# Moving loads of S, own rows and the diagonal to GpSimd's queue, two writes to ScalarE's, and dealing the first layer out sooner

## The chip, the cores and the metric

The kernel runs on one core of a Trainium2 chip. The metric is the device time of one execution in microseconds, given as the median of several runs. The core has five engines that each run their own instruction list in order: TensorE (PE in the profile; its weight loads are PEld), VectorE (DVE), ScalarE (ACT), GpSimd (POOL) and SyncE (SP). Transfers are issued by an engine's list and are carried out by 16 DMA engines that all lists share. In the profile the list of SP is SPq.

## The reference, cut to what matters

The input x has 32 batches of 512 nodes with 256 features; adj is one sparse 512 x 512 matrix whose pattern is symmetric. Four layers follow one another. The first and the last have this form:

```python
pre_u = einsum('bud,dk->buk', h_t, W1[:d])
pre_v = einsum('bvd,dk->bvk', h_t, W1[d:])
hidden = relu(pre_u[:, :, None, :] + pre_v[:, None, :, :] + b1)
S = sigmoid(einsum('buvk,ko->buvo', hidden, W2)[..., 0] + b2[0])
a_t = einsum('buv,bud->bvd', S * A_a, h_t)
m_t = einsum('uv,bud->bvd', A_m, h_t) * h_t
z_t = beta1*h_t + beta2*(a_t @ Wa + ba) + beta3*(m_t @ Wm + bm)
```

Both matrices A_a and A_m are adj, so S is needed only where adj is not zero. The second layer is z + relu(adj z W + b); the third is an attention layer over all 512 x 512 pairs, with adj added to its logits.

## The kernel before

The 32 batches are worked in 8 groups of 4 (t = 0 to 7). For each group, and for the first layer ("0") and the last ("3") apart, there is a table in device memory with the rows pre_u and pre_v of every node for the 4 batches (2 MB), and a grid "cells" of 512 x 512 x 4 values of S * adj, in two halves.

**The streams.** `sparse_path` gives each group five streams of pieces, each a Python generator:

- `first` (21 pieces): loads h, transposes it into hT (`turned`, L537), writes hT to xT in device memory (L730), and in `pre` makes the table rows (L549 on DVE, L550 on ACT) and writes them (table<-puv, L557).
- `edges` of layer 0: works through ITEMS = 36 lists of 128 adjacency entries. Each item fetches 128 rows of the table by an indirect DMA on GpSimd (rows<-table, L582), adds the node's own rows (`mine`, a plain load of 512 KB, L622, four per run, in DVE L654), forms relu times W2 and sums it (DVE L667), takes the sigmoid and puts 128 x 4 values into cells by an indirect DMA on GpSimd (cells<-s, L576). Each put waits until the put before it to the same half has landed. The diagonal of cells is written apart (`own_1`, L606).
- `middle`: loads S * adj from cells (SA, four loads of 1 MB, `load`, L689), then goes through the 4 batches: rest of layer 0, layers 1 and 2, the table of layer 3. It writes x2T (L876) and x2 (L888). The attention's output is yT, in two halves (DVE L874), and `pre` of layer 3 needs both of them.
- `edges` of layer 3, and `last`: the rest of layer 3, which loads SA again, and x2 and x2T, and writes the output.

**Their order.** `weave` sorts all pieces by a due time in units of one group and emits them in that order. Pieces of kind "fill" (`first`, `last`) are held back, up to HELD = 8 of them while a `middle` runs, and are let out at places that `middle` marks. The order on each engine is then set by the framework's scheduler, which goes by its own estimates of time. An instruction that waits holds up everything behind it on its engine, and the same holds for the DMA issues in an engine's list.

**Who issues what.** In the kernel before, SP issues every plain transfer. GpSimd issues only the indirect ones. Buffers that matter here: hT has one buffer, which `first` and `last` share; puv has three, `mine` three, rows five, SA four for each layer.

For t from 2 on, `first` and then `edges` of layer 0 of group t come before its `start`, while `middle` of group t-1 runs; `edges` of layer 3 and `last` of a group come behind its `end`, as the numbers `early` and `behind` tell. So during `middle` of group t-1 the run of `edges` of layer 3 of group t-2 comes first, and that of layer 0 of group t follows it.

There is also a dense path for matrices with too many entries; it is not taken here.

Of the kernel before, what the change touches and what calls it, by code (L numbers as in the profile page):

```python
# [16 lines left out]
P = 128  # L17
# [28 lines left out]
class Model:  # L46
# [37 lines left out]
    def load(self, name, shape, view, pool=None):  # L84
        t = (pool or self.const).tile(shape, F32, name=f"w_{name}")
        self.nc.scalar.dma_start(t, view)
        return t
# [327 lines left out]
class Sparse:  # L415
# [24 lines left out]
    def psum(self):  # L440
        return self.ps.tile([P, N], F32, name="pst", tag="pst")
# [144 lines left out]
    def edges(self, g, spare=()):  # L586

        nc, e, w = self.nc, self.e, g.w  # L590
        flat = "p c b -> p (c b)"
        own = g.self_s.rearrange(flat)
        ready, fetched = [], {}
        lead = LEAD + len(spare) - 1 if spare else LEAD
        tags = [None] * 5 + list(spare)
        mine = {}
        places = g.table.rearrange("(c p k) n -> c k p n", p=P, k=2)

        def own_1():
            self.sigmoid_of(own)  # L600
            diag = self.counts.diag.unsqueeze(2).to_broadcast([P, NC, NB])
            nc.vector.tensor_tensor(g.self_s, g.self_s, diag, ALU.mult)
            for q in range(2):
                diagonal = g.cells[q][q * HALF : q * HALF + HALF * (N + 1), :]
                diagonal = diagonal.rearrange("(c p a) b -> p c a b", p=P, a=N + 1)[:, :, 0, :]
                nc.sync.dma_start(diagonal, g.self_s[:, 2 * q : 2 * q + 2, :])  # L606

        def run_1(ks):
            self.sigmoid_of(g.s[:, ks, :].rearrange(flat))
            value = e.value[:, ks].unsqueeze(2).to_broadcast([P, ks.stop - ks.start, NB])  # L610
            nc.vector.tensor_tensor(g.s[:, ks, :], g.s[:, ks, :], value, ALU.mult)
            for k in range(ks.start, ks.stop):
                j = e.order[k]
                ready.append((e.half_of(j), e.cell[:, j : j + 1], g.s[:, k, :]))

        def fetch(n):
            j = e.order[n]
            c = j // OWN
            if c >= NC or c not in mine:
                t = self.gath.tile([P, GROUP], F32, name="mine", bufs=3)  # L620
                if c < NC:
                    nc.sync.dma_start(t, places[c, 0])  # L622
                    mine[c] = t
                else:
                    self.fetch(t, g, e.iu[:, j - NC * OWN : j - NC * OWN + 1])
            else:
                t = mine[c]
            if tag := tags[n % len(tags)]:
                rows = self.act.tile([P, GROUP], F32, name="rows_more", tag=tag)
            else:  # L630
                rows = self.gath.tile([P, GROUP], F32, name="rows")
            self.fetch(rows, g, e.iv[:, j : j + 1])
            fetched[n] = rows, t

        def put():

            at = next((n for n, r in enumerate(ready) if r[0] != self.half), 0)
            if ready:
                r = ready.pop(at)
                self.half = r[0]  # L640
                self.put(g, *r)

        self.half = 1
        for n in range(lead):
            fetch(n)
        yield

        todo = [(2, lambda: self.exp_of(w, own)), (4, own_1)]
        done = 0
        for k in range(ITEMS):  # L650
            for _ in range(2 if spare and len(ready) > 2 else 1):
                put()
            rows, other = fetched.pop(k)
            nc.vector.tensor_tensor(rows, rows, other, ALU.add)  # L654
            if k + lead < ITEMS:
                fetch(k + lead)
            if spare:
                by_entry = rows.rearrange("p (b d) -> p b d", b=NB)
                w2 = w["W2bc"].unsqueeze(1).to_broadcast([P, NB, D])
                nc.vector.scalar_tensor_tensor(by_entry, by_entry, 0.0, w2, ALU.max, ALU.mult)  # L660
            for b in range(NB):
                part = rows[:, b * D : (b + 1) * D]
                at = g.s[:, k, b : b + 1]
                if spare:
                    nc.scalar.activation(part, part, AF.Identity, accum_out=at)
                else:
                    nc.vector.scalar_tensor_tensor(part, part, 0.0, w["W2bc"], ALU.max, ALU.mult, accum_out=at)  # L667
            if k % 4 == 3 or k >= ITEMS - 3:
                ks = slice(done, k + 1)
                near = spare or k >= ITEMS - 5  # L670
                todo.append((k + (1 if near else 3), lambda ks=ks: self.exp_of(w, g.s[:, ks, :].rearrange(flat))))
                todo.append((k + (1 if near else 4), lambda ks=ks: run_1(ks)))
                done = k + 1
            while todo and todo[0][0] <= k:
                todo.pop(0)[1]()
            yield
        for _, f in todo:
            f()
        while ready:
            put()  # L680
        yield

    def load(self, g, layer):

        tiles = []
        for c in range(NC):
            t = self.act.tile([P, N, NB], F32, name=f"SA{layer}", bufs=NC)
            cells = g.cells[c // 2][c % 2 * P * N : (c % 2 + 1) * P * N, :]
            self.nc.sync.dma_start(t.rearrange("p v b -> p (v b)"), cells.rearrange("(p v) b -> p (v b)", p=P))  # L689
            tiles.append(t)  # L690
        return tiles

# [24 lines left out]
    def first(self, g, i):  # L717


        def load(b):  # L720
            h = self.act.tile([P, NC, D], F32, name="h0", tag="h", bufs=2)
            self.nc.sync.dma_start(h, self.xr[i + b])
            return h

        h = load(0)
        for b in range(NB):
            ahead = load(b + 1) if b < NB - 1 else None
            hT = self.turned(h, "hT0", "hT")
            yield
            self.nc.sync.dma_start(self.xT[i + b], hT)  # L730
            yield from self.pre(g, b, hT)
            h = ahead
        self.settle()
# [53 lines left out]
    def middle_one(self, g0, g3, b, i, SA, keep, given):  # L787
        nc, m, w = self.nc, self.m, g0.w
        act, small, psum = self.act, self.small, self.psum
        h, hT, hWa, flat = keep  # L790
# [89 lines left out]
        for c in range(0, NC, 2):  # L880
            pt = psum()
            for k in range(2):
                for d in range(DC):
                    at = k * D + d * P
                    nc.tensor.transpose(pt[:, at : at + P], xT[:, d, (c + k) * P : (c + k + 1) * P], m.ident)
            x2 = small.tile([P, 2, D], F32, name="x2", tag="ex", bufs=4)
            nc.scalar.copy(x2, by_two(pt))
            nc.sync.dma_start(self.x2s[i][:, c : c + 2, :], x2)  # L888
            yield

    def put_back(self, eT, ic, ex):
# [116 lines left out]
def sparse_path(ctx, m, counts, xr, outr, B):  # L1008
# [10 lines left out]
    for t in range(last + 1):  # L1019
        g0, g3 = Group(sp, m.g0, f"0_{t}"), Group(sp, m.g3, f"3_{t}")  # L1020
        start, end = (max(0.0, k - 0.47) for k in (t, t + 1))
        behind = (end, end + 0.48), (end + 0.52, end + 1.2)
        if t == 0:
            early = (-0.385, -0.30), (-0.292, -0.02)
        elif t == 1:
            early = (-0.28, -0.06), (0.02, start - 0.04)
        else:
            early = (start - 0.8, start - 0.54), (start - 0.53, start - 0.05)
        if t == last - 1:
            behind = (end, end + 0.46), (end + 0.6, end + 1.08)  # L1030
        if t == last:
            end -= 0.2
            behind = (end, end + 0.46), (end + 0.29, end + 0.45)
        streams += [
            (sp.first(g0, t * NB), FIRST, *early[0], "fill"),
            (sp.edges(g0, ("yT", "mhT3") if t == 0 else ()), EDGES, *early[1], ""),
            (sp.middle(g0, g3, t * NB), middle_shares(t == 0), start, end, "main"),
            (sp.edges(g3, ("yT", "h1", "hT1") if t == last else ()), EDGES, *behind[0], "free"),
        ]
        if t == 0:  # L1040
            streams.append((sp.middle_before(g0, 0), AHEAD, -0.15, -0.03, ""))
        if t < last:
            streams.append((sp.last(g3, t * NB), LAST, *behind[1], "fill"))
        else:
            streams.append((sp.last_before(g3, t * NB), AHEAD, *behind[1], ""))
            streams.append((sp.last_behind(g3, t * NB), BEHIND, end + 0.5, end + 0.6, ""))
# [235 lines left out]
```

## Time and profile before

| | |
|---|---|
| median of 3 runs | 3247.94 us (3246.24 to 3251.05) |
| profiled execution | 3230.9 us, span from first to last instruction 3229.2 us |
| PE / DVE / POOL / ACT busy | 2773.2 / 2371.6 / 1488.3 / 1007.0 us |
| mean granted TensorE clock | 0.928 |
| DMA by GpSimd's queue / SP's queue | 338.90 MB / 334.68 MB |
| busy share of the 16 DMA engines, same queues | 32.8% / 31.0% |

One period of the steady state is about 371 us. In it PE is busy for nine tenths of the time, and DVE is full while an `edges` run is on. Lines such as L557 are lines of the kernel before; the change keeps the line numbers. In a list of waits, "A <- B: x, n, y" says that A waited for B for x us in all, n times, at most y us. In the chain of waits each row has its start, its length and what ran or was waited for.

### The profile page before, as it was taken

The numbers are of one execution on the slowest core, as the hardware profiler recorded it, in microseconds if no ns is written. First come the engines' busy times: TensorE is split into PE (matmuls) and PEld (weight loads), VectorE is DVE, ScalarE is ACT, GpSimd is POOL, SyncE is SP. The second block draws the span as 40 slices with busy tenths as digits, with TensorE's granted clock in tenths as the row PEclk, the third lists the DMA queues.
The fourth block names the chain that finished last, engine by engine and source line by source line (L and its number), as shares of the span: only waits on it lengthen the run. The fifth ranks groups of instructions, "written<-read, shape, count | busy, mean of one in ns | idle before, by whom it ended". The sixth has DMA issues, their size and how long they took to land.

```text
span 3229.2 us, 32451 instructions
## 1 busy us (share of the span) xinstructions
PE 2773.2 (86%) x8646; PEld 1656.2 (51%) x8646; DVE 2371.6 (73%) x7692; ACT 1007.0 (31%) x2341; POOL 1488.3 (46%) x1248
## 2 busy tenths in 40 slices
PE   6346887989997999979999899979998899999947
PEld 3223444546554566435654565536654465545626
DVE  7777736989596976969598786969688695953662
ACT  4452333322233222333223232333223222232441
POOL 1565402747264543636354462636355362630371
PEclk9677898999999999989999999989999999999969
DMA  8876425777567766776577766776577765640663
GB/s 273 295 246 229 152 91 166 261 262 224 188 226 240 234 196 202 249 241 220 173 230 235 245 203 211 237 250 207 178 219 246 242 221 190 219 159 33 209 201 112
DMA packets 302718, 679.40 MB, mean 210 GB/s; under 512 B 52672, under 2 KB 170944, under 8 KB 294336
## 3 DMA queue, kind: packets, MB, share of 16 engines
q0 software_dynamic: 111168, 338.90, 32.8%
q1 hardware_dynamic: 186224, 334.68, 31.0%
q10 hardware_dynamic: 5136, 3.68, 0.4%
q8 instruction: 71, 1.16, 0.1%
q14 instruction: 119, 0.97, 0.1%
HBM read 531.12 MB, written 146.01 MB: 210 GB/s over the span
## 4 chain that ended last, share of the span: by engine, by line
PE 38%; DVE 34%; DMA 17%; issue 6%; ACT 3%; POOL 1%; SPq 0%; ACTq 0%; POOLq 0%; DVEq 0%
PE pst L43 28%; DVE rows L667 11%; DVE rows L654 10%; DMA rows<-table,iv 6%; DMA table<-puv 4%; PE pst L945 4%; PE pst L802 2%; DMA cells<-s,cell 2%; PE pst L954 1%; DVE ex L852 1%; PE pst L896 1%; DMA cells<-self_s 1%; PE pst L809 1%; DVE ex L854 1%; DMA mine<-table,iu 1%
## 5 line engine op out<-in xcount | busy, mean ns | idle before, releaser
L582 POOL DMA_INDIRECT rows<-table,iv x554 | 680.1, 1228 | 1047.4 <-DMA table<-puv 383.1
L576 POOL DMA_INDIRECT cells<-s,cell x576 | 684.3, 1188 | 592.7 <-DMA cells<-s,cell 357.0
L654 DVE TENSOR_TENSOR rows<-rows,mine 128x1024 f32<-128x1024 f32 x554 | 667.3, 1215 | 195.0 <-DMA rows<-table,iv 178.9
L667 DVE SCALAR_TENSOR_TENSOR rows<-rows,L_gnn_W2bc 128x256 f32<-128x256 f32 x2016 | 750.9, 413 | 0.4
L43 PE MATMUL pst<-adj,h 128*128 128x512 f32 x1024 | 453.5, 592 | 0.0
L43 PE MATMUL pst<-L_gnn_Wa,hT 128*128 128x256 f32 x1024 | 260.6, 408 | 142.4 <-DMA hT<-xT 69.4
L43 PE MATMUL pst<-w_L_gnn_W,hT 128*128 128x512 f32 x512 | 261.2, 646 | 57.4 <-ACT hT L537 46.3
L43 PEld LDWEIGHTS pst<-adj,h 128*128 128x128 f32 x1024 | 192.8, 190 | 219.5 <-issue 214.1
L43 PEld LDWEIGHTS pst<-L_gnn_Wa,hT 128*128 128x128 f32 x1024 | 207.8, 208 | 187.8 <-issue 103.2
L43 PE MATMUL pst<-w_L_gnn_W,yT 128*128 128x512 f32 x512 | 239.9, 622 | 66.0 <-DVE yT L874 66.0
L43 PE MATMUL pst<-eT,feats 128*128 128x512 f32 x512 | 240.0, 624 | 9.1 <-ACT eT L897 9.1
L43 PE MATMUL pst<-adjT,zW 128*128 128x512 f32 x512 | 225.9, 592 | 0.0
L550 ACT COPY puv<-pst 128x256 f32<-128x256 f32 x256 | 94.7, 372 | 412.5 <-DVE puv L549 376.2
L945 PEld LDWEIGHTS pst<-hWa,SA 128*128 128x128 f32 x896 | 213.4, 328 | 5.9 <-issue 3.3
L945 PE MATMUL pst<-hWa,SA 128*128 128x256 f32 x896 | 216.2, 397 | 0.0
L43 PEld LDWEIGHTS pst<-w_L_gnn_W,yT 128*128 128x128 f32 x512 | 101.8, 200 | 196.3 <-issue 111.0
L549 DVE TENSOR_TENSOR puv<-pst,bc_L_gnn_b 128x256 f32<-128x256 f32 x256 | 106.6, 417 | 127.4 <-PE pst L43 64.4
L771 ACT COPY flat<-SA 128x512 f32<-128x512 f32 x128 | 134.5, 1122 | 203.3 <-PE pst L43 178.8
L802 PE MATMUL pst<-flat,hWa 128*128 128x512 f32 x448 | 196.8, 592 | 0.0
L43 PEld LDWEIGHTS pst<-w_L_gnn_W,hT 128*128 128x128 f32 x512 | 102.0, 206 | 168.0 <-issue 90.5
L43 PE MATMUL pst<-WT,hT 128*128 128x256 f32 x512 | 141.8, 434 | 38.8 <-DVE hT L810 38.8
L896 PE MATMUL pst<-ident,ex 128*128 128x128 f32 x512 | 88.5, 302 | 99.2 <-DVE ex L857 62.6
(167 smaller groups left out, 3728.0 us busy)
## 6 DMA issues: line engine op xcount, KB each, us to landing
table<-puv SPq DMA_DIRECT2D x256, 256.0 KB, 4.9
SA<-cells SPq DMA_DIRECT2D x64, 1024.0 KB, 7.0
h<-in_x_dram SPq DMA_DIRECT2D x64, 512.0 KB, 6.6
mine<-table SPq DMA_DIRECT2D x64, 512.0 KB, 6.2
hT<-xT SPq DMA_DIRECT2D x36, 512.0 KB, 5.0
h<-x2s SPq DMA_DIRECT2D x36, 512.0 KB, 6.1
xT<-hT SPq DMA_DIRECT2D x32, 512.0 KB, 7.5
x2T<-yT SPq DMA_DIRECT2D x32, 512.0 KB, 5.0
```

The source lines that it names most:

```text
L43: nc.tensor.matmul(out, lhsT, rhs, start=(n == 0), stop=(n == len(pairs) - 1))
L549: nc.vector.tensor_tensor(puv[:, 0, :], pp[:, 0:D], w["b1bc"], ALU.add)
L550: nc.scalar.copy(puv[:, 1, :], pp[:, D:])
L576: self.nc.gpsimd.indirect_dma_start(out=g.cells[half], out_offset=bass.IndirectOffsetOnAxis(ap=at, axis=0), in_=s, in_offset=None)
L582: self.nc.gpsimd.indirect_dma_start(out=rows, out_offset=None, in_=g.table, in_offset=bass.IndirectOffsetOnAxis(ap=at, axis=0))
L654: nc.vector.tensor_tensor(rows, rows, other, ALU.add)
L667: nc.vector.scalar_tensor_tensor(part, part, 0.0, w["W2bc"], ALU.max, ALU.mult, accum_out=at)
L771: self.nc.scalar.copy(flat[:, r, :], SA[r][:, :, b])
L802: nc.tensor.matmul(pz, hWa[:, r, cs], flat[:, r, :], start=(r == 0), stop=False)
L809: nc.tensor.matmul(pz, w["Wm"][:, d, cs], mhT[:, d, :], start=False, stop=(d == DC - 1))
L896: nc.tensor.transpose(pt[:, js], ex[:, js], self.m.ident)
L945: nc.tensor.matmul(pz[:, k * D : (k + 1) * D], SA[r][:, cs, b], hWa[:, r, :], start=(r + k == 0), stop=False)
```

## The change

Five issues change their engine, and two numbers of the order change. 160 transfers go from SP to GpSimd (64 loads of SA, 64 of `mine`, 32 of the diagonal) and 96 from SP to ScalarE (32 writes of xT, 64 of x2). `first` of group t >= 2 gets due times 0.06 of a group sooner, and `last` has to be through 0.07 of a group sooner.

```diff
-                nc.sync.dma_start(diagonal, g.self_s[:, 2 * q : 2 * q + 2, :])
+                nc.gpsimd.dma_start(diagonal, g.self_s[:, 2 * q : 2 * q + 2, :])
...
-                    nc.sync.dma_start(t, places[c, 0])
+                    nc.gpsimd.dma_start(t, places[c, 0])
...
-            self.nc.sync.dma_start(t.rearrange("p v b -> p (v b)"), cells.rearrange("(p v) b -> p (v b)", p=P))
+            self.nc.gpsimd.dma_start(t.rearrange("p v b -> p (v b)"), cells.rearrange("(p v) b -> p (v b)", p=P))
...
-            self.nc.sync.dma_start(self.xT[i + b], hT)
+            self.nc.scalar.dma_start(self.xT[i + b], hT)
...
-            nc.sync.dma_start(self.x2s[i][:, c : c + 2, :], x2)
+            nc.scalar.dma_start(self.x2s[i][:, c : c + 2, :], x2)
...
-        behind = (end, end + 0.48), (end + 0.52, end + 1.2)
+        behind = (end, end + 0.48), (end + 0.52, end + 1.13)
...
-            early = (start - 0.8, start - 0.54), (start - 0.53, start - 0.05)
+            early = (start - 0.86, start - 0.6), (start - 0.53, start - 0.05)
```

## The prediction

> **What bounds the kernel now.** I read the page first: busy times, then the chain that ended last.
>
> ```profile
> PE 2773.2 (86%) x8646; PEld 1656.2 (51%) x8646; DVE 2371.6 (73%) x7692; ACT 1007.0 (31%) x2341; POOL 1488.3 (46%) x1248
> ...
> PE 38%; DVE 34%; DMA 17%; issue 6%; ACT 3%; POOL 1%; SPq 0%; ACTq 0%; POOLq 0%; DVEq 0%
> ```
>
> PE is nearest to a bound, with 456 us idle in 3229.2 us. No queue move makes PE's work smaller, so a gain can only come out of that idle time. Busy time by stretches puts 146 us of it into the first 320 us (set-up) and 63 us into the last 209 us. In the steady state it sits in one place per group: where `edges` of layer 3 ends and `edges` of layer 0 of the next group but one begins. Six such stretches of 56 us:
>
> ```profile
> 1005.00:1061.00 56.00, 38.24 (x109) 20.23 (x108) 25.95 (x90) 18.36 (x38) 12.74 (x13) 0.82 0.77 256
> 1376.00:1432.00 56.00, 37.06 (x108) 19.71 (x107) 25.98 (x90) 18.27 (x38) 14.21 (x14) 0.82 0.79 252
> ...
> sum 336.00, PE 238.46 PEld 126.02 DVE 171.57 ACT 111.70 POOL 92.17; mean PE 39.74 PEld 21.00 DVE 28.59 ACT 18.62 POOL 15.36
> ```
>
> The first figure after the length is PE's busy time: 97.5 us idle in the six, while DVE is half idle too. So nothing is full there; something is late. The chain of waits for 1372 to 1430 us says what:
>
> ```profile
> 1381.40 7.69 DMA cells<-s,cell
> ...
> 1389.36 5.29 DMA cells<-s,cell
> ...
> 1395.39 4.27 DMA cells<-s,cell
> ...
> 1400.41 2.12 DMA cells<-s,cell
> 1402.55 0.33 SPq L689
> ...
> 1403.58 6.82 DMA table<-puv
> 1410.41 0.33 SPq L622
> ...
> 1410.79 4.23 DMA cells<-self_s
> 1415.02 8.83 DMA rows<-table,iv
> 1423.87 1.24 DVE rows L654
> ```
>
> Four puts into one half go one after the other; SP's list has stood at the SA load (L689) for them; only then do table writes, `mine` and the diagonal leave; then come the first gather, its DVE add, and behind that the second half of yT, for which PE has run dry. The waits of the whole run, PE's and SP's own, agree:
>
> ```profile
> PE pst L43 <- DVE yT L874: 66.0, 7, 12.5
> ...
> PE pst L43 <- ACT hT L537: 46.3, 23, 6.9
> ```
>
> ```profile
> SPq L689 <- DMA cells<-s,cell: 337.8, 30, 24.3
> ```
>
> Six of the seven yT waits (9.2 to 12.5 us) lie in the six stretches. There PE also waits 24.8 us in five of them for hT, which ACT cannot overwrite until the xT write has landed; at 1382.37 that write left directly behind the SA load, 7.9 us after its data were made.
>
> **The change part by part.**
>
> *SA off SP, `first` sooner (the six stretches).* 0.06 of 371 us is 22 us, so the table could be written before the last puts. In the order of the changed kernel as built, GpSimd's list there reads for t = 3 to 7: last put of half 0, two SA loads, put, `mine`, put, `mine`, put, two gathers, the fourth put, more gathers (for t = 2, the first stretch, the SA loads come later; I count it alike). The first gather thus follows three puts, not four, and no table write, `mine` or diagonal behind them. With the times above, the third put left at 1395.39. The added issues ahead of it are two SA and two `mine`; the nearest row is a GpSimd gather's issue, 1.23 us plus a gap of 0.30, so 4 x 1.53 = 6.1 us. Third put at 1401.5, gather a put's issue and gap later at 1402.8, landed 8.8 us later at 1411.6, against 1423.87. But DVE's order also changes: the second half of yT now stands behind the third item's add, and that item's gather behind the fourth put: put 5.0 us after the third, as 1400.41 stands to 1395.39 (1406.5), gather 1407.8, landed 1416.6, add 1.24, yT 0.75: 1418.6. Before, PE went on at 1426.3. Gain 7.7, taken as 8 us in each stretch, 6 x 8 = 48 us. The 24.8 us for xT are not added: that stall ends before the chain of puts does, and turns into waiting for it. Ends: nothing gained if the puts land as late as 7.7 us each; all of 66.0 + 24.8 = 91 us if the table's lead carries through.
>
> *160 issues on GpSimd.* At 1.53 us they are 245 us over the span, on an engine that idles 1741 us; per period 31 us beside 184 us busy in 375. Hidden as issues; if that cover went they would cost up to 245. A row shows how they stretch: gathers issued at 1237 to 1242, before DVE's L667 start, took 0.94 us; at 1245 to 1261, beside them, mostly 1.68. In the Trainium skill, "SBUF — State Buffer", section on a bandwidth-pool intuition that's wrong, VectorE and GpSimd lock each other out of a shared port, and a GpSimd transfer that takes about 620 ns alone takes about 3100 ns beside a copy on VectorE. By that rule, as an estimate, the 160 issues would cost 160 x 2.5 = 400 us more of GpSimd's time. By the row of this trace the stretch is 160 x 0.74 = 118 us, part of which the mean of 1.23 already holds.
>
> *Start of layer 3's runs.* There SP isn't late: table<-puv at 1228.62 (4.50 us), gather at 1236.98, DVE's wait 4.5 to 5.4 us in each of six. Now three `mine` stand ahead of the first gather on GpSimd; two of them can leave while the last table rows are still landing. Between 0 and 3 x 1.53 = 4.6 us; I take 1.5, since the chunks land about as far apart as an issue lasts. Seven runs: +10 us (0 to 32).
>
> *The diagonal and set-up.* Diagonals landed 15.72 us after 98.57, in SP's queue behind 512 KB writes of zeros, and the first put waited 13.7 us for them. On GpSimd they are clear of those; typical landing is 7.4 us: 8.3 us sooner, but SA loads and diagonals of group 1 then stand between gathers, one wait of a landing (7.0 us). I take -5 (-8 to +7).
>
> *The tail.* SA loads at 3159.01 and 3172.88 are on the path to the last sums. On GpSimd two of them stand between the last puts: 2 x 1.53 = 3.1. The three `mine` ahead of the first gather at 3023 add up to 4.6, of which I take 2: +5 us (+3 to +8).
>
> *96 writes on ACT.* An SP issue lasts 0.32 to 0.6 us; 96 x 0.5 = 48 us on an engine that is 69% idle, and each follows ACT's own copy. Hidden beside PE and DVE; uncovered it is 48. Some of these wait for an earlier SP transfer to land before they leave; by the built order that is one issued some eight transfers before, so 0.
>
> *`last` sooner, and SP's other transfers* (h, x2T, the output) that no longer queue behind SA: the work only moves inside stretches where PE and DVE are both full, and none of these transfers is a long wait of the steady state: 0 (-10 to +10).
>
> Sum: -48 + 10 - 5 + 5 = -38 us against the profiled execution's 3230.9 us, so 3193; the three runs' median lies 17 us above that, and the same difference from it is 3210 us.
>
> Against the whole change speaks a rule. In this trace SP's `mine` landed in 6.2 us (median), and GpSimd's gathers of the same 512 KB in 6.2 too. The Trainium skill, "DMA: Bandwidth & Descriptors", puts plain loads on SP and only indirect ones on GpSimd (section Issuing engine by pattern), with first bytes after about 0.6 and 1 us (Specifications). By that, 160 x 0.4 is an estimate of 64 us if every load were on the path, and the sum would be +26.
>
> **The rivals.**
>
> *R1, all of it.* The table's lead frees the stretches: -91 - 8 + 10 + 5 = -84: 3164 us. For it: DVE and PE are half empty there. Against it: the chain of puts stays, now with SA loads between them.
>
> *R2, slower: GpSimd's single list becomes the late one.* Gathers wait behind SA loads that wait for puts, and behind their megabytes in the same queue. In layer 0's runs the last two SA loads stand among the gathers, after six of them. Rows have five buffers, and an item takes DVE 1.21 + 4 x 0.41 = 2.9 us, so 14 us are covered; it decides from where the SA loads hold the gathers for longer than that. If the queue is served in order, 2 x 7.0 us of landing plus a put's 5 us is 19 us, 5 too many, in 8 runs: 40. Layer 3's 8 runs start 3 us later (of 0 to 4.6): 24. With the tail's 5, and the stretches giving back only half of 48: 40 + 24 + 5 - 24 = +45: 3293 us. For it: the new order has these waits. Against: GpSimd idles 13.6 us at just this place now.
>
> *R3, no change.* The puts, not SP, set the end of the stretch, and what the table gains is idled away: 3248 us.
>
> **How the numbers follow.** Forecast (gain of 10 to 65 us) 0.45, R1 0.20, R2 0.27, R3 0.08. 0.2% is 6.5 us, about what a measurement of this kernel can tell. Faster 0.65, same 0.08, slower 0.27. The range 3150 to 3280 leaves out the far ends of R1 and R2, together about 0.2; the forecast alone spans 3183 to 3238.
>
> **What would show it.** Right: SP's wait at L689 gone; PE's wait for yT falls from 66.0 to below 40 us and its wait for hT behind xT from 24.8 to near 0; periods of 363 us. Wrong: DVE's wait for gathers (178.9 us now) grows, with GpSimd standing at L689 or L622 in mid-run; ACT standing at L730 or L888; or periods of 371 us or more.

## The result and the profile after

| | before | after |
|---|---|---|
| median of 12 runs each, side by side | 3247.0 us | 3246.47 us (3238.74 to 3255.63) |
| ratio | | 1.0003, 95% interval 0.9992 to 1.0013 |
| profiled execution, span | 3230.9, 3229.2 us | 3248.3, 3246.6 us |
| PE / DVE / POOL busy | 2773.2 / 2371.6 / 1488.3 us | 2786.7 / 2361.8 / 1557.7 us |

No change that can be measured. The forecast was 3210 us; the time lies within its range, but not where the likeliest case had it. Before's profiled execution lay some 16 us under its median and after's 2 us over, so the two profiles differ by 18 us more than the kernels do: a group of a profile says where time went, but not to the last 15 us.

The page of the changed kernel, busy times and then the chain that ended last:

```profile
PE 2786.7 (86%) x8645; PEld 1649.0 (51%) x8646; DVE 2361.8 (73%) x7692; ACT 1003.5 (31%) x2341; POOL 1557.7 (48%) x1408
...
DVE 38%; PE 25%; DMA 21%; issue 9%; ACT 4%; POOL 3%; ACTq 0%; POOLq 0%; SPq 0%; DVEq 0%
```

PE has as much idle time as before (460 us; it was 456). The chain has moved from PE to DVE and DMA. PE's waits over the whole run (us, times, longest):

```profile
PE pst L43 <- DVE yT L874: 53.3, 11, 10.9
...
PE pst L43 <- ACT hT L537: 27.2, 21, 3.0
...
PE pst L896 <- ACT hWa L702: 15.4, 9, 2.4
...
PE pst L809 <- DVE mhT L712: 14.1, 12, 2.0
```

The wait for yT fell from 66.0 to 53.3 us and not below 40; the wait for hT from 46.3 to 27.2. The last two lines are new: before they were 1.5 us and nothing. On DVE's side, its waits for what it adds in L654:

```profile
DVE rows L654 <- DMA rows<-table,iv: 216.0, 57, 17.6
...
DVE rows L654 <- DMA mine<-table,iu: 38.5, 13, 7.1
```

They were 178.9 and 15.8. SP's 337.8 us at L689 are gone.

The six stretches again, each laid so that the first add of layer 0's run stands where it stood in the windows of before (columns as there):

```profile
1367.60:1423.60 56.00, 42.64 (x125) 21.59 (x124) 37.57 (x142) 20.78 (x44) 30.74 (x31) 0.91 0.76 242
...
sum 336.00, PE 259.79 PEld 131.88 DVE 237.20 ACT 125.95 POOL 188.68; mean PE 43.30 PEld 21.98 DVE 39.53 ACT 20.99 POOL 31.45
```

PE is idle for 76.2 us of them, where it was 97.5: the stretches gave 21 us, not 48. The chain of waits in one of them (start, length, what):

```profile
1397.39 8.60 issue
...
1406.23 2.14 DMA cells<-s,cell
...
1414.32 6.75 DMA rows<-table,iv
...
1421.09 1.22 DVE rows L654
1422.32 0.66 DVE yT L874
```

The 8.60 us are one put on its way. GpSimd's own timeline names it:

```profile
1394.09 1.32 POOL L689 DMA_DIRECT2D SA<-cells  x2 [1.94 <-PE pst L896]
1395.71 1.13 POOL L576 DMA_INDIRECT cells<-s,cell  x1 [0.30 <-DVE both L552]
...
1406.23 1.01 POOL L576 DMA_INDIRECT cells<-s,cell  x1 [8.84 <-DMA cells<-s,cell]
...
1409.13 1.02 POOL L576 DMA_INDIRECT cells<-s,cell  x1 [1.34 <-DMA cells<-s,cell]
1410.46 0.98 POOL L582 DMA_INDIRECT rows<-table,iv  x1 [0.30 <-issue]
...
1413.00 1.01 POOL L576 DMA_INDIRECT cells<-s,cell  x1 [0.30 <-issue]
```

The put at 1395.71 stands behind two SA loads of 1 MB in its own queue and lands after 10.25 us. It is the first of the last four puts, and before the first of these took 7.69 us. The four together did not get slower: from the issue of the first to that of the fourth it is 17.3 us here and was 19.0; over the five stretches from t = 3 on, 13.4 to 17.3 against 18.6 to 19.7. Counted from the end of layer 3's run (its last L654), the first gather leaves after 24.4 us, where it was 40.5; that is more than the 12.2 us by which the prediction had it leave sooner.

PE still waits, because DVE's order is another. Before, DVE made the first half of yT well ahead of the first add of layer 0's run, which began at 1423.87:

```profile
1409.89 0.75 DVE L874 SCALAR_TENSOR_TENSOR yT<-pst,col_L_gnn_bias,yT 128x512 f32<-128x512 f32 x1 [2.88 <-PE pst L43]
```

In the changed kernel that first half stands behind the add, for whose rows DVE waits, and PE waits with it (the bracket gives the idle time before the row and what ended it):

```profile
1415.48 1.23 DVE L654 TENSOR_TENSOR rows<-rows,mine 128x1024 f32<-128x1024 f32 x1 [16.26 <-DMA rows<-table,iv]
1416.62 0.75 DVE L874 SCALAR_TENSOR_TENSOR yT<-pst,col_L_gnn_bias,yT 128x512 f32<-128x512 f32 x1
```

```profile
1417.42 5.44 PE L43 MATMUL pst<-w_L_gnn_W,yT 128*128 128x512 f32 x6 [9.62 <-DVE yT L874]
```

This order, the first half behind one add and the second behind three, stands in all five stretches; with the old due times of `first` it is none and one. In the six stretches PE's wait for yT fell from 65.8 to 52.1 us only.

Where the 21 us and more went back is seen when a period is cut at the `edges` runs: first to last L654 of a run, and the gaps between. Worked out from the L654 rows and PE's busy time between them, mean of five periods:

| length us (PE idle us) | before | after | all queue changes, `first` sooner, `last` as before |
|---|---|---|---|
| layer 3's run | 129.8 (10.9) | 135.2 (9.5) | 132.6 (6.4) |
| gap to layer 0's run | 49.6 (14.6) | 29.5 (9.6) | 30.8 (8.8) |
| layer 0's run | 126.7 (5.4) | 139.1 (10.7) | 133.3 (11.0) |
| gap to layer 3's run | 64.6 (0.5) | 68.9 (2.0) | 67.4 (0.5) |
| period | 370.7 (31.4) | 372.7 (31.9) | 364.1 (26.7) |

The gap fell by 20 us per period; the runs and the other gap took 22 back. Part of that is only DVE and PE work that moved out of the gap, which is why the last column has it too and is yet 8.6 us shorter. (Its profile comes from a chip on which the kernel before takes 3230.5 us, 0.5% less than beside the changed kernel, so some 2 of the 8.6 us are the chip's; PE's idle time, 26.7 against 31.9 us, is the safer measure.) That column is an experiment, told below: the gain of the forecast, without one line of the change.

### The profile page after: what moved, and what is told of

Same layout as the page of the kernel before. It is cut to its first block, busy times and chain, and to the rows that moved or that the text cites. A ratio compares the mean times of both kernels' runs of the same rounds, so it can differ in the third digit from the quotient of the medians.

```text
span 3246.6 us, 32347 instructions
## 1 busy us (share of the span) xinstructions
PE 2786.7 (86%) x8645; PEld 1649.0 (51%) x8646; DVE 2361.8 (73%) x7692; ACT 1003.5 (31%) x2341; POOL 1557.7 (48%) x1408
## 4 chain that ended last, share of the span: by engine, by line
DVE 38%; PE 25%; DMA 21%; issue 9%; ACT 4%; POOL 3%; ACTq 0%; POOLq 0%; SPq 0%; DVEq 0%
PE pst L43 19%; DVE rows L667 13%; DVE rows L654 12%; DMA rows<-table,iv 6%; DMA table<-puv 6%; PE pst L945 3%; DMA cells<-s,cell 2%; DMA mine<-table,iu 2%; POOL cells L576 2%; DVE puv L549 1%; DVE ex L852 1%; DVE mhT L712 1%; ACT flat L771 1%; PE pst L802 1%; DVE ex L854 1%
## 5 line engine op out<-in xcount | busy, mean ns | idle before, releaser
L582 POOL DMA_INDIRECT rows<-table,iv x554 | 665.2, 1201 | 435.0 <-DVE rows L667 229.0
L654 DVE TENSOR_TENSOR rows<-rows,mine 128x1024 f32<-128x1024 f32 x554 | 667.9, 1217 | 255.0 <-DMA rows<-table,iv 216.0
L43 PE MATMUL pst<-adj,h 128*128 128x512 f32 x1024 | 452.4, 593 | 0.0
L43 PE MATMUL pst<-L_gnn_Wa,hT 128*128 128x256 f32 x1024 | 259.2, 407 | 124.9 <-DMA hT<-xT 74.4
L43 PEld LDWEIGHTS pst<-adj,h 128*128 128x128 f32 x1024 | 193.0, 191 | 216.6 <-issue 212.9
L43 PEld LDWEIGHTS pst<-L_gnn_Wa,hT 128*128 128x128 f32 x1024 | 206.9, 207 | 171.9 <-issue 103.5
L43 PE MATMUL pst<-w_L_gnn_W,yT 128*128 128x512 f32 x512 | 240.1, 622 | 53.4 <-DVE yT L874 53.3
L43 PE MATMUL pst<-w_L_gnn_W,hT 128*128 128x512 f32 x512 | 250.2, 623 | 24.6 <-ACT hT L537 24.2
L43 PE MATMUL pst<-eT,feats 128*128 128x512 f32 x512 | 241.4, 627 | 13.5 <-ACT eT L897 13.5
L622 POOL DMA_DIRECT2D mine<-table x64 | 36.1, 566 | 443.6 <-DMA table<-puv 215.8
L43 PE MATMUL pst<-adjT,zW 128*128 128x512 f32 x512 | 225.4, 594 | 3.2 <-ACT zW L822 3.2
L945 PEld LDWEIGHTS pst<-hWa,SA 128*128 128x128 f32 x896 | 214.4, 328 | 8.7 <-issue 5.0
L945 PE MATMUL pst<-hWa,SA 128*128 128x256 f32 x896 | 216.3, 398 | 0.0
L43 PEld LDWEIGHTS pst<-w_L_gnn_W,yT 128*128 128x128 f32 x512 | 100.6, 199 | 188.6 <-issue 106.8
L567 ACT ACTIVATE s<-s,L_gnn_nb 128x16 f32<-128x16 f32 (+2 forms) x176 | 53.4, 304 | 462.4 <-DVE rows L667 459.5
L43 PE MATMUL pst<-WT,hT 128*128 128x256 f32 x512 | 147.8, 443 | 52.7 <-DVE hT L810 52.4
```

The lines of the kernel that those rows point to most:

```text
L43: nc.tensor.matmul(out, lhsT, rhs, start=(n == 0), stop=(n == len(pairs) - 1))
L567: self.nc.scalar.activation(t, t, AF.Exp, bias=w["nb2"], scale=-1.0)
L582: self.nc.gpsimd.indirect_dma_start(out=rows, out_offset=None, in_=g.table, in_offset=bass.IndirectOffsetOnAxis(ap=at, axis=0))
L622: nc.gpsimd.dma_start(t, places[c, 0])
L945: nc.tensor.matmul(pz[:, k * D : (k + 1) * D], SA[r][:, cs, b], hWa[:, r, :], start=(r + k == 0), stop=False)
```

## The experiments

18 kernels. Ratios are to the kernel before, timed on the same chip at the same time; 1% is 32 us.

**1. Queues and due times apart.** Theory A was that SA's bytes ahead of the puts eat the gain, B that the DMA engines are full in any case, C that the puts set the end.

```diff
# due times only (before, plus)
+        behind = (end, end + 0.48), (end + 0.52, end + 1.13)
+            early = (start - 0.86, start - 0.6), (start - 0.53, start - 0.05)
# queues only: the change without these two lines
```

> The kernel before with nothing but the three new due times; all queues as before. Theory A (the bytes of SA, ahead of the last puts on GpSimd's queue, eat what the sooner table brings: in the changed kernel the put behind two SA loads landed after 10.25 us, where the same put of before took 4.27): here SA stays on SP, so the gain of the sooner table stays, as far as SP's list, which stands at the SA load up to 24.3 us, lets it: 5 to 30 us under before. Theory B (the 16 DMA engines are full in the stretch, share 1.00 to 1.05 for 10 to 20 us, so the order of issue can't matter): within 5 us of before. Theory C (queues and due times each gain nothing, the puts set the end of the stretch): within 5 us too.

> The changed kernel with the due times of before; the five queue changes stay. Theory A: SA's bytes ahead of the puts, and the table no sooner, so nothing pays for them: 6 stretches by 4 to 6 us, 24 to 36 us over before. Theory B: within 5 us of before. Theory C: within 5 us.

Due times alone: 1.0003 (0.9989 to 1.0017). Queues alone: 0.9959 (0.9941 to 0.9977). The queue changes gain 13 us when left alone, against A, and the due times take them back; for that no theory was on the table.

**2. SA's place, and SA's bytes.**

```diff
-            self.nc.gpsimd.dma_start(t.rearrange("p v b -> p (v b)"), cells...)
+            self.nc.sync.dma_start(t.rearrange("p v b -> p (v b)"), cells...)
# a quarter of the bytes, in load and sums:
+            n = N if layer == 0 else P
+            t = self.act.tile([P, n, NB], F32, name=f"SA{layer}", bufs=NC)
...                                                  (and [:, : n * NB] in the load)
-                        pz[:, k * D : (k + 1) * D], SA[r][:, cs, b], ...
+                        pz[:, k * D : (k + 1) * D], SA[r][:, 0:P, b], ...
```

> The changed kernel with the SA loads alone back on SP; own rows and diagonal on GpSimd, xT and x2 on ScalarE, due times as changed. Theory A: the put that landed in 10.25 us lands in about 4 to 5 again, the first gathers leave some 5 us sooner, and SP's list stands at SA behind table writes that are out already: 20 to 40 us under the changed kernel. Theory B: the same megabytes pass in the same stretch, so the changed kernel's time within 5 us. Theory C: within 5 us.

> The changed kernel with the four SA loads of layer 3 cut to a quarter of their bytes each (256 KB for 1 MB; the sums of the last layer read the same 128 columns again, so part of S is left out and the output is not the reference's); instructions, matmuls, queues and waits stay. 3 MB less in each stretch, at the 370 GB/s of the full engines 8 us. Theory A and theory B both expect it faster than the changed kernel, A by the put's 6 us in six stretches (about 36 us), B by up to 8 us in six (about 50). Theory C (puts and PE's own work set the time): within 10 us.

> The kernel before with the four SA loads of layer 3 cut to a quarter of their bytes (the last layer's sums read the same 128 columns again, so part of S is left out); the same cut made the changed kernel 44 us faster. Theory A (SA's bytes hurt only where they share GpSimd's queue with the puts): on SP's queue they stand ahead of no put, so 0 to 15 us under before. Theory B (the DMA engines are full in the stretch, whichever queue the bytes are in): about the same 44 us, 30 to 55 under before.

> The kernel before with the SA loads alone on GpSimd; own rows, diagonal, xT and x2 stay on SP, due times as before. With SA back on SP the changed kernel became about 22 us slower, and all five queue changes under the old due times were 13 us faster than before. Theory D (SA's place is the only queue change that counts, since SP's list no longer stands for the puts): 10 to 25 us under before. Theory E (it counts only together with own rows on GpSimd, which keeps them from standing behind table writes): within 6 us of before, or slower.

SA back on SP in the changed kernel: 1.0063 (1.0042 to 1.0085), slower by 20 us, so A is false there, and B, which had said within 5 us, missed too. A quarter of the bytes, which leaves three quarters of layer 3's S out of the sums: 0.9865 (0.9841 to 0.9888) with SA on GpSimd, 0.9875 (0.9854 to 0.9896) with all on SP. Some 40 us in either queue, which is what B had said and A had not. In the changed kernel the cut left the lists of PE, DVE, ACT and SP in the same order, as the traces show, and 16 of GpSimd's 1408 issues in another; so there it is the bytes, if not those few issues. In the kernel before, 310 of DVE's 7692 instructions came in another order with it, so that its 40 us are not shown to be the bytes alone. The place of SA counts as well: SA alone on GpSimd is 0.9943 (0.9925 to 0.9962), 18 us, as theory D had it.

**3. The two due times apart.**

```diff
# first sooner, last as before (queues changed; then also with all queues of before)
-        behind = (end, end + 0.48), (end + 0.52, end + 1.13)
+        behind = (end, end + 0.48), (end + 0.52, end + 1.2)
# last sooner, first as before
-            early = (start - 0.86, start - 0.6), (start - 0.53, start - 0.05)
+            early = (start - 0.8, start - 0.54), (start - 0.53, start - 0.05)
```

> All five queue changes and of the due times only the sooner first (0.86 and 0.6); last keeps its old end (1.2). All queue changes with the old due times were 13 us faster than before, with both new due times equal to before. If the sooner first is what costs (its table writes and h loads come into the run of edges that still goes on): equal to before, within 5 us. If the denser last is what costs (fill pieces pressed into a shorter stretch): 8 to 18 us under before.

> All five queue changes and of the due times only the denser last (end + 1.13); first keeps its old due times. Theory F (the denser last is a cost of its own: 32 of a group's 128 sum matmuls leave the stretch around the end of layer 0's run, where PE waits for DVE and the puts anyway, for the middle of the period, where PE is full): 0.7 to 1.3% over the queue changes alone, which stood at 0.9959 of before, so 1.003 to 1.009 of before. Theory G (it costs only together with the sooner first, since both are pressed together): within 0.2% of the queue changes alone, 0.994 to 0.998.

> The kernel before, all on SP's queue as it was, with only the sooner first. With both new due times it stood at 1.0003 of before. Theory F: the sooner first gains by itself and the denser last had eaten it: 0.985 to 0.994 of before. If the sooner first needs the queue changes (SP's list stands at SA for the puts before it sends the table writes): within 0.2% of before.

| | due times of before | `first` sooner | `last` sooner | both |
|---|---|---|---|---|
| queues of before | 1 | 0.9920 (0.9906 to 0.9934) | not run | 1.0003 |
| queues changed | 0.9959 | **0.9885 (0.9863 to 0.9906)** | 1.0038 (1.0025 to 1.0050) | 1.0003 |

This settles the sum. `first` sooner gains 0.7 to 0.8%, 24 to 26 us, with either set of queues. The queue changes gain 0.4%, 13 us. `last` sooner costs 0.8% with the old `first` and 1.2% with the sooner one, 26 to 38 us (0.8% with the sooner `first` and the queues of before). The best kernel, at 0.9885, is the change without its 1.13; it beats both. In the traces the sooner `first` puts some 250 of PE's 8646 matmuls in another place of its list, the sooner `last` 860 to 990.

**4. What in the sooner `last` costs.** The first three of the four stretches of one period, cut at the copies of f (L835), columns as in the windows above. The changed kernel:

```profile
1570.50:1667.70 97.20, 92.20 (x293) 58.10 (x292) 63.79 (x199) 24.71 (x45) 35.87 (x34) 0.96 0.59 193
1667.70:1750.80 83.10, 80.34 (x254) 43.59 (x254) 78.85 (x285) 29.80 (x63) 50.92 (x43) 1.00 0.79 256
1750.80:1852.10 101.30, 82.43 (x236) 44.54 (x235) 75.13 (x265) 26.78 (x56) 52.63 (x49) 0.90 0.74 233
```

The best kernel (the change without its 1.13):

```profile
1547.50:1634.60 87.10, 84.96 (x278) 51.59 (x277) 55.76 (x172) 25.81 (x48) 29.73 (x28) 1.00 0.62 206
1634.60:1728.10 93.50, 89.04 (x285) 51.88 (x284) 87.71 (x311) 30.20 (x62) 57.84 (x48) 0.98 0.76 247
1728.10:1820.50 92.40, 77.42 (x221) 39.83 (x220) 71.01 (x255) 27.21 (x56) 48.87 (x47) 0.93 0.74 240
```

The same stretches for L945 alone, the sums of `last` (PE busy and count, then PEld). The changed kernel:

```profile
1570.50:1667.70 97.20, 15.40 (x64) 15.24 (x64) 0.96 0.59 193
1667.70:1750.80 83.10, 0.00 (x0) 0.00 (x0) 1.00 0.79 256
1750.80:1852.10 101.30, 3.88 (x16) 3.88 (x16) 0.90 0.74 233
```

The best kernel:

```profile
1547.50:1634.60 87.10, 7.88 (x32) 7.70 (x32) 1.00 0.62 206
1634.60:1728.10 93.50, 7.63 (x32) 7.54 (x32) 0.98 0.76 247
1728.10:1820.50 92.40, 0.00 (x0) 0.00 (x0) 0.93 0.74 240
```

In the changed kernel 32 of the 128 sums have left the second stretch for the first, and 16 have come into the third, which holds the end of layer 3's run and the puts. As a mean of four periods the first stretch is 6.3 us longer than in the best kernel (95.7 against 89.4), and the second and third together are 2.5 us longer too (187.1 against 184.6; of the two differences the chip makes up 0.5 and 0.9 us), though 16 matmuls fewer run in them. Work taken from there saved nothing; where it went it cost. That left two questions: is it the tail (32 sums) or the front (16 sums)? And is there more to gain by going the other way?

```diff
# last later:                    (end + 0.52, end + 1.27), first sooner
# first sooner still:            (start - 0.92, start - 0.66), last to end + 1.2
# tail alone, start moved too:   (end + 0.56, end + 1.13)
# front alone, start moved too:  (end + 0.49, end + 1.2)
# tail alone, start kept:        (end + 0.52, end + 1.13), shares [1.157] * 8 + even(25)
# front alone, start kept:       (end + 0.52, end + 1.2), shares [0.869] * 8 + even(25)
```

> All queue changes, the sooner first, and last let out later than ever (end + 1.27 for 1.2 and 1.13). With 1.13 it stood at 1.0003 of before, with 1.2 at 0.9885. Theory F, if still more of last's PE work can lie in the part of the period that DVE and the puts set: another 5 to 15 us, 0.984 to 0.987. If that part is full at 1.2: 0.987 to 0.992. If it only matters that last's end lies over the start of first: 0.987 to 0.990.

> All queue changes, last's old end (1.2), and first sooner by another 0.06 (0.92 and 0.66). The sooner first by 0.06 took the queue changes from 0.9959 to 0.9885. If the table's lead still sets the end of the stretch: again 10 to 25 us, 0.981 to 0.985. If the puts and the DMA engines set it now: 0.986 to 0.991. Over that, if the sooner first takes PE work out of the part where PE has room: above 0.991.

> The changed kernel, but last starts later (end + 0.56 for end + 0.52) and still ends at end + 1.13: its first sums stay behind the first f1 copy of the stretch, as with 1.2, while its tail stays as sooner as in the changed kernel. If the tail is what costs (PE work taken from where PE waits anyway): 0.996 to 1.003 of before, as the changed kernel. If the front is what costs: 0.986 to 0.991, as the kernel with the end at 1.2. Half each: about 0.994.

> All queue changes, the sooner first, last from end + 0.49 (for 0.52) to the old end + 1.2: its front comes even a little sooner than in the changed kernel, its tail as in the kernel that gained (0.9885). If the front is what costs: 0.996 to 1.003. If the tail is what costs: 0.986 to 0.991.

> The changed kernel (end + 1.13) with the first 8 of last's 33 pieces spaced as in the kernel that gained and the other 25 crowded, so that the tail is sooner and the front and the SA loads stand where they stood there. If the tail is what costs: 0.997 to 1.003 of before. If the front: 0.986 to 0.991. If any move of last costs (the gain is one of a good fit of the order, not of one place): above 0.993.

> All queue changes, the sooner first, last to its old end (1.2) with only the first 8 of its 33 pieces spaced as in the changed kernel. If the front is what costs: 0.997 to 1.003. If the tail: 0.986 to 0.991. If any move of last costs: above 0.993, here and with the tail crowded.

| | ratio | PE waits L809 for mhT | PE waits L43 for hT L537 |
|---|---|---|---|
| best kernel | 0.9885 | 1.0 us | 11.9 us |
| the change (both ends sooner) | 1.0003 | 14.1 | 27.2 |
| tail, start moved | 1.0003 (0.9987 to 1.0019) | 9.9 | 27.9 |
| front, start moved | 1.0042 (1.0025 to 1.0060) | 14.7 | 30.6 |
| tail, start kept | 0.9981 (0.9965 to 0.9997) | 19.2 | 20.6 |
| front, start kept | 0.9991 (0.9980 to 1.0002) | 15.2 | 23.8 |
| `last` later | 0.9941 (0.9924 to 0.9958) | 7.6 | 21.9 |
| `first` sooner still | 0.9980 (0.9966 to 0.9995) | 10.0 | 16.5 |

Neither end is the cause alone: each end by itself costs the whole gain, and so does, by half, moving `last` the other way. So the account by moved sums is not enough, and the last expectation of the six, that any move of `last` costs, is the one that held. What the four kernels with one end moved share with the changed one is in the last two columns: PE stands for an ACT copy of `first` (L537) and a DVE product (L712) that are not yet made when it comes to them. The two waits are 13 us in the best kernel and 38 to 45 us in those five, 25 to 32 of the 31 to 51 us between them. They show where PE's time goes with the sooner `first`, and not more: with the old `first` and the sooner `last` (1.0038) they are 21 us. Nor is a wait that falls a gain by itself: with the due times alone (1.0003) PE's waits for yT and for hT are 57 us less than before, and its idle time is 470 us against 456. Why one order of fill pieces has these waits covered, and a shift of either end uncovers them, was not settled.

**5. Which queue changes the sooner `first` needs**, in the best kernel, and own rows also in the changed one:

```diff
# SA back on SP
-            self.nc.gpsimd.dma_start(t.rearrange("p v b -> p (v b)"), cells...)
+            self.nc.sync.dma_start(t.rearrange("p v b -> p (v b)"), cells...)
# own rows and diagonal back on SP
-                    nc.gpsimd.dma_start(t, places[c, 0])
+                    nc.sync.dma_start(t, places[c, 0])
-                nc.gpsimd.dma_start(diagonal, g.self_s[:, 2 * q : 2 * q + 2, :])
+                nc.sync.dma_start(diagonal, g.self_s[:, 2 * q : 2 * q + 2, :])
```

> The kernel that gained (all queue changes and the sooner first, 0.9885) with SA alone back on SP. If SP's list, standing at SA for the puts, was what held the first gathers: 0.5 to 1% slower than 0.9885, so 0.993 to 0.999. If the sooner table alone makes up for it (with every queue as before it gave 0.9920): 0.986 to 0.992.

> The kernel that gained (0.9885) with own rows and the diagonal back on SP. In the changed kernel the same step cost 1.7% (1.0170 for 1.0003). If own rows on SP stand behind table writes that wait for the landing of others, that holds here too: 1.000 to 1.010. If that cost belonged to the denser last: 0.985 to 0.992.

> The changed kernel with own rows and the diagonal back on SP; SA stays on GpSimd, xT and x2 on ScalarE, due times as changed. If own rows on GpSimd hold its gathers up (issues and waits for the table in its single list, DVE's wait for gathers grew from 178.9 to 216.0 us): 5 to 25 us under the changed kernel. If own rows on GpSimd are what lets the first gathers leave early: 5 to 25 us over it. If they are hidden, as the forecast took them: within 5 us.

SA back: 0.9886 (0.9866 to 0.9906), no difference at all. SP's waits in that kernel:

```profile
SPq L689 <- DMA cells<-s,cell: 365.4, 30, 25.6
```

PE's waits in it:

```profile
PE pst L43 <- DVE yT L874: 38.9, 15, 4.4
```

SP stands at SA for 365 us, more than the 337.8 of before, and it costs nothing: the table is written already (where the third SA load of a group left at 1405.96 us, the last table write ahead of it left at 1395.87). In the changed kernel SP stood there for 498 us with SA back, and that cost 20 us. The wait for yT is even lower (38.9 us; 55.0 with SA on GpSimd), and DVE's wait for the first gather of layer 0's runs, from t = 3 on, is 9.4 to 10.0 us there and 14.3 to 15.5 in the best kernel. Yet the gather does not come sooner: counted from the end of layer 3's run it leaves after 26.1 to 27.7 us there and after 24.9 to 25.9 in the best kernel. DVE stands less because it has more to do ahead of that add, which itself begins after 32.8 to 34.2 us, against 30.4 to 31.6.

Own rows back: 1.0005 (0.9993 to 1.0017) in the best kernel, 1.0170 (1.0145 to 1.0194) in the changed one. PE's waits in the best kernel with own rows on SP:

```profile
PE pst L43 <- DVE yT L874: 91.0, 9, 18.1
```

DVE's waits in it:

```profile
DVE rows L654 <- DMA rows<-table,iv: 264.4, 42, 24.8
```

That first gather is now waited for 22 to 25 us, and the first of layer 3's runs 10 to 12 (3 to 5 in the best kernel). The first gather of layer 0's runs leaves 32.8 to 35.0 us after the end of layer 3's run. So own rows and the diagonal have to go to GpSimd with the other queue changes, and SA does not. The sooner table by itself needs neither: with all queues as before, own rows on SP, it gained 0.8% (0.9920).

None of these edits moves transfers alone, for the scheduler orders each kernel anew. Read from the traces, PE's list stays nearly as it was (0 to 13 of 8646 matmuls in another place), but between two kernels that differ in queues alone 256 to 978 of DVE's 7692 instructions stand elsewhere. What a queue is worth under one fixed order was not tested.

The writes on ScalarE were never run alone. An xT write is issued in 0.33 us, and the 29.5 us in which ACT waited for its landing before (hT L537) are gone in the changed kernel.

## Why the prediction was right and wrong

**The step that failed** is "*`last` sooner, and SP's other transfers* ... the work only moves inside stretches where PE and DVE are both full ...: 0 (-10 to +10)". It measured +38 us in this kernel (1.0003 against 0.9885) and +26 with the old `first`. Neither half of the reason held: the work did not stay inside full stretches, and an order of pieces that is denser is not neutral where PE is full. That it takes away what stood between a producer on ACT or DVE and its matmul fits the two waits of the table, and is not shown to be the cause. A due time was costed like a queue, by what it delays; it should have been costed by the order that results, which was there to be read: 32 sums on another side of a `middle` batch. Without that step the sum was -38 us; without that edit the kernel measured -37 us (0.9885).

**That sum was right in size, but not for its reasons,** so its size was luck. Term by term:

- *SA off SP, `first` sooner: -48.* Two edits in one term. `first` is worth 24 to 26 us by itself; SA's move, on top of it, nothing. "SP's list has stood at the SA load" was true and not the cause: the same wait stands at 365 us in a kernel of the same speed. In the changed kernel the stretches gave 21 us in PE's idle time, not 48, though the gather left sooner than forecast: the prediction had read in the new order that the second half of yT stands behind an add, and not that the first half now does too, for which PE waits 9.62 us. And the steady state's idle time does not sit in that one place: the six stretches held 97.5 of the 247 us between 320 and 3020 us.
- *"The 24.8 us for xT are not added."* It was the larger part of what fell: PE's wait for hT went from 46.3 to 11.9 us in the best kernel, that for yT from 66.0 to 55.0 only.
- *160 issues on GpSimd: hidden.* Nothing speaks against it (SA's 64 back on SP left the best kernel's time as it was), and their price was set too high: 64 `mine` at 0.57 us (mean), 64 SA at 0.58 (median), 32 diagonals at 0.78 are 98 us, not 245, and POOL's busy time rose by 69. The trace has no sign of plain issues five times longer beside DVE, as "SBUF — State Buffer" in the Trainium skill has it for copies on VectorE (section on the bandwidth-pool intuition): the longest `mine` issue is 0.85 us. But only 9 of DVE's instructions here are copies, so the rule itself is not tested.
- *Start of layer 3's runs: +10.* DVE's wait for the first gather went from 4.5 to 6.2 us to 5.3 to 6.4, in the mean 0.6 per run, 5 in all. Within its bounds.
- *Diagonal and set-up: -5.* PE's idle time in the first 320 us went from 146.1 to 143.4 us. *Tail: +5.* From the last f to the end 248.1 and 248.6 us: nothing.

**The rivals.** R3 named the result and not the mechanism: the table's gain is not idled away, it is 0.8%. R2's mechanism is there (178.9 to 216.0 us of waits for gathers, puts behind SA) but SA on GpSimd loses nothing: SA back on SP gives the same time in the best kernel and a slower one in the changed kernel. R1 did not come.

**The rules that spoke against.** "DMA: Bandwidth & Descriptors" in the Trainium skill puts plain loads on SP ("Issuing engine by pattern"). Here `mine` landed in 5.7 us from GpSimd and 6.2 from SP, and taking it back to SP with the diagonal costs 1.2% in the best kernel. That what a load stands behind in its list counts, and not the queue's own latency, fits this; DVE's order changed with it, so it is not shown. The same page ("Queues, rings and completion order") has each DMA engine go round the queue rows packet by packet; megabytes would then delay most what shares their queue. That agrees with 10.25 us for the put behind SA on GpSimd, where the same put took 7.69 us with SA on SP. The support is weak: in the one other stretch of the changed kernel whose trace has this landing it is 6.4 us.

## What to carry to other kernels

Cost a change of due times by the instruction order it makes, not by the sign of the shift: count which filler matmuls change sides, what then stands between each small copy and the matmul that reads it, and which small operations have come behind an instruction that waits for a transfer. A long wait in one queue's list is worth only what stands behind it in that list; look whether that could leave sooner by itself before moving the waiting transfer. When a change of several edits comes out at nothing, time them apart first: here +38, -13 and -25 us made a zero.

## What the hardware showed that was not expected

Beside the landing of a put behind SA (a median of 3.6 us over the changed kernel, 10.25 there, its longest), it is the price of bytes, as far as order is not part of it: 3 MB fewer per group in layer 3's SA gave 40 to 44 us over 8 groups, 5 us per group, with SA in SP's queue as in GpSimd's. Where the puts wait, from 1399 to 1404 us of the changed kernel, the DMA engines' share is 1.00 at 370 GB/s (the last two figures of the row); 3 MB are 8 us at that rate.

```profile
1399.00:1404.00 5.00, 3.96 (x12) 2.05 (x13) 0.22 (x1) 0.58 (x1) 0.00 (x0) 1.00 1.00 370
```

Fewer bytes there are worth more than the five queue changes together, which gave 13 us.
